# Cross-attention of a decoder block in turns of four heads: interleaved key and value chains, half-product queries, a ring of six PSUM banks

## The chip, the core and the metric

The kernel runs on one core of one Trainium2 chip. The metric is device time in microseconds (us) of one execution, the median of several runs. The engines, and how the profile names them: PE (TensorE, matmuls; PEld is its loading of weights), DVE (VectorE), ACT (ScalarE), POOL (GpSimd) and SP (SyncE, whose queue issues all the DMAs). Each engine takes its instructions in order and waits on semaphores for the others. PE writes its results into PSUM, which has 8 banks; the kernel gives a tile of PSUM one bank or more. Everything else lies in SBUF.

## The reference

The reference is one decoder block of three sublayers on `x` (8 batches, 224 rows, 512 columns), each followed by `x = layernorm(x + sublayer(x))`: a self-attention with normalised heads, a cross-attention over `ctx` (8 batches, 750 rows, 384 columns), and a gated feed-forward whose weights are rounded to -1, 0 and 1 times a scale. The change lies in the cross-attention:

```python
q = split_heads(x @ Wq)          # 16 heads of 64
k = split_heads(context @ Wk)
v = split_heads(context @ Wv)
sim = jnp.einsum('bhid,bhjd->bhij', q, k) * SCALE
attn = jax.nn.softmax(sim, axis=-1)
out = jnp.einsum('bhij,bhjd->bhid', attn, v)
return out.transpose(0, 2, 1, 3).reshape(b, sq, HEADS * DIM_HEAD) @ Wo + bo
```

All of it is in float32, but for the feed-forward's matmuls.

## The kernel before

The kernel has three stages: self-attention (to about 490 us), cross-attention (to about 1480 us) and feed-forward. In each stage the instructions of PE, DVE, ACT and POOL keep the order in which the source writes them (`manual_schedule`); the order of SP's queue is the framework's own, which also puts in all semaphore waits. A tile of a pool with one buffer may be written anew only when all its readers are done.

**Units.** The cross-attention runs over 64 units: 8 batches, and in each 8 pairs of heads (`units`, L1219). One pass of the loop at L1250 writes this order:

1. `scores` (L1060): for each of 6 chunks of 125 context rows and each of the two heads, one matmul of keys by queries. Two chunks of one head share a PSUM bank, so a unit takes 6 banks. ACT copies each bank to `cpT` (L1081), and from the second two chunks on DVE also reads the bank, for the running maximum (L1083). L1087 leaves the maximum per context row in `cmx`.
2. `across` (L1092): about a dozen small DVE instructions that take the maximum over the context rows, together with the sums of the unit before (`csm`), and leave the negated maxima and the inverse sums in `mx_n`. `negated_maxima` spreads the maxima over a PSUM bank.
3. one step of `weight_steps` (below).
4. `weighted` of the unit before (L1161): 12 matmuls of values by exponentials into one bank, `ov_c`.
5. the first part of a chain of products (`turn_products`): in odd passes the keys, in even ones the values, of four heads of one batch. A chain writes a 2 x 2 block matrix product as seven half-size products (`half_products`, L251) with a third inner block; it uses three PSUM banks, x, z and w, of which x is used four times over. ACT moves five of the results out, POOL adds two, DVE one (L301).
6. ACT's deferred half of the weight step (`acts`).
7. `queries` of the next unit (L1045): four matmuls of 224 columns, moved out by ACT with the scale.
8. `exponentials` (L1143): for each head DVE adds the negated maxima (L1147), ACT takes the exponential (L1155), POOL sums over the chunks (L1157 to L1159).
9. the rest of the chain, and then `normalise` of the unit before, which reads `ov_c` straight from PSUM (L1187).
10. loads of weight blocks for the next chains (`load_blocks`), context loads and sums a batch ahead, layernorm work, and the output projection of a finished tile of 128 rows (`cross_finish`, 16 matmul records of 512 columns).

**Banks.** The pool `c_mm` has 7 banks, handed out in order to score banks, spread maxima, queries, chain banks, transposes and projections; `ov_c` has the eighth.

**Weight steps.** The feed-forward's weights are brought in beside the cross-attention. In chunks of 2048 columns, two slots of `w_stage` in turn: first every chunk is loaded and its absolute values summed on ACT (L914); then every chunk is loaded again and in halves of 1024 columns scaled and rounded on ACT (L937), clipped on DVE (L940), converted on ACT (L947) and stored to DRAM (L948). One step goes with each unit, but for a few, until it is done.

**Weights.** All of `xattn_Wq` lies in SBUF. Blocks of key and value weights stream through `xw`, with sums of blocks that POOL formed during self-attention (`room_sums`, L138).

Of the kernel before, what the change touches and what calls it, by code (L numbers as in the profile page):

```python
# [38 lines left out]
HID = 2048  # L39
# [13 lines left out]
QH = 4  # L53
NCHUNK = 4
CHUNK = DIM * HID // P // NCHUNK
PIECE = 1024
# [9 lines left out]
def decoder_block(ctx: ExitStack, tc: tile.TileContext, a: dict, out: bass.AP):  # L66
# [95 lines left out]
    room_steps = room_sums(0), room_sums(1)  # L162
# [159 lines left out]
    with tc.tile_pool(name="a_sb", bufs=2) as sb, tc.tile_pool(  # L322
# [335 lines left out]
        ctx_even = xw = bo = None  # L658
# [3 lines left out]
        CTX = KC * SC + 4 * HALF  # L662
        contexts = {}

        def open_context(b, t):
            contexts[b] = (
                t[:, : KC * SC].rearrange("p (k r s) -> p k r s", k=KC, r=2),
                t[:, KC * SC :].rearrange("p (i s) -> p i s", i=4),
            )
# [7 lines left out]
        def sum_context(b, i):  # L677
# [4 lines left out]
                (s[:, 2], c[:, 0, 0], c[:, 0, 1], ALU.subtract),  # L682
                (s[:, 3], c[:, 1, 0], s[:, 1], ALU.subtract),
# [3 lines left out]
        def load_blocks(j, g):  # L687
# [8 lines left out]
            nc.sync.dma_start(out=xw[:, j, KC + 2 :], in_=sums_w[:, j, g])  # L696

# [28 lines left out]
        for m in range(NS):  # L726
# [25 lines left out]
            for _ in range({10: 1, 11: 1, 12: 1, 13: 2, 15: 1, 16: 1, 17: 1, 18: 2}.get(m, 0)):  # L752
                next(room_steps[m // 15])
            next(sums)
# [37 lines left out]
            if m == 13:  # L792
                room_load(1)
            if m == NS - 3:
# [4 lines left out]
                xwq = wpool.tile([P, KD, INNER], F32, tag="w", name="xattn_Wq")  # L799
# [4 lines left out]
                nc.sync.dma_start(  # L804
                    out=xwq, in_=a["xattn_Wq"].rearrange("(k p) n -> p k n", p=P)
                )
# [77 lines left out]
    with tc.tile_pool(name="c_sb", bufs=2, reuse_waits="tile") as sb, tc.tile_pool(  # L884
        name="c_mm", bufs=7, space=PSUM, reuse_waits="tile"
    ) as ps_mm, tc.tile_pool(
        name="c_ov", bufs=1, space=PSUM, reuse_waits="tile"
    ) as ps_ov, tc.manual_schedule(engines=ENGINES):
        ctx_odd = sb.tile([P, CTX], F32, name="ctx_odd", bufs=1)
# [5 lines left out]
        stage = sb.tile([P, 2, CHUNK], F32, name="w_stage", bufs=1)  # L895
        oT = sb.tile([P, NPAIR, RING], F32, name="coT", bufs=1)


        mx = sb.tile([P, 2, S], F32, name="cmx", bufs=1)
        nc.vector.memset(mx, -3.0e38)  # L900
        csm = sb.tile([P, 2, S], F32, name="csm", bufs=1)
        nc.vector.memset(csm, 0.0)
        xT = {}

        def stage_chunk(i, c, s):
            name = ("w_gateT", "w_upT", "w_downT")[i]
            kk = (HID // P if i == 2 else KD) // NCHUNK
            nc.sync.dma_start(
                out=stage[:, s, :].rearrange("p (k n) -> p k n", k=kk),
                in_=a[name].rearrange("(k p) n -> p k n", p=P)[:, c * kk : (c + 1) * kk, :],  # L910
            )
# [22 lines left out]
        def weight_round(i, c, s, h):  # L934

            piece = stage[:, s, h * PIECE : (h + 1) * PIECE]
# [3 lines left out]
            return lambda: nc.vector.tensor_scalar(  # L940
# [3 lines left out]
        def weight_store(i, c, s, h):  # L944
            piece = stage[:, s, h * PIECE : (h + 1) * PIECE]
            w = sb.tile([P, PIECE], BF16, name="w_t", bufs=1)
            nc.scalar.activation(w, piece, AF.Identity, bias=unrounder)  # L947
            nc.sync.dma_start(  # L948
                out=ternary[i][:, c, h * PIECE : (h + 1) * PIECE], in_=w
            )  # L950
# [9 lines left out]
        def weight_steps():  # L960
# [3 lines left out]
            for n, (i, c) in enumerate(chunks):  # L964
# [3 lines left out]
                acts.append(partial(weight_sum, i, c, n % 2))  # L968
# [3 lines left out]
            before = None  # L972
            for n, (i, c) in enumerate(chunks):
                for h in range(CHUNK // PIECE):
                    yield
                    if before:
                        weight_store(*before)
                    if h == 0 and n + 1 < len(chunks):
                        stage_chunk(*chunks[n + 1], (n + 1) % 2)
                    before = (i, c, n % 2, h)  # L980
                    acts.append(lambda at=before: late.append(weight_round(*at)))
            yield
            weight_store(*before)

        def transpose_x(b):

            for i in needs[b]:
# [5 lines left out]
                for pb, c, at, n in pieces(i):  # L993
                    if pb not in xT:
                        xT[pb] = sb.tile([P, KD, S], F32, name="xT")
                    nc.scalar.copy(xT[pb][:, :, c : c + n], tr[:, :, at : at + n])

        VN = QH * DH

        def products_kv(b, j, product, dest):

            c, sums = contexts[b]
            b11, b21, b31, b22, b32, t1, t2, t3, t4n, dif = (
                xw[:, j, i] for i in range(KC + 2 + NSUM)
            )
            like = lambda t: shaped(t, j)  # L1010
            part = lambda name: like(sb.tile([P, HALF + 9], F32, name=name, bufs=1))
            return half_products(
                product,
                [[c[:, k, r] for k in range(2)] for r in range(2)],
                ((b11, None), (b21, b22)),
                [sums[:, i] for i in range(4)],
# [233 lines left out]
        for n in range(-1, len(units)):  # L1250
# [12 lines left out]
            for f in acts:  # L1263
                f()
# [268 lines left out]
```

## Time and profile before

| quantity | value |
|---|---|
| median of 3 runs | 1639.58 us (1639.06 to 1640.03) |
| the profiled execution | 1638.94 us |
| its span, first to last instruction | 1637.2 us |
| granted TensorE clock, mean | 0.999 of full speed |
| busy PE, DVE, ACT, POOL | 1617.3, 1340.3, 984.7, 908.9 us |
| cross-attention, 495 to 1480 us: busy PE, DVE, ACT, POOL | 980.8, 813.7, 615.0, 571.6 us |
| PE start to start of a unit, value chain and key chain | 13.81 us (897.53 to 911.34), 13.53 us (911.34 to 924.87) |

The profile is a record of one execution. Busy time is the time in which an engine had an instruction under way; a matmul's end is modelled, so where matmuls follow each other the time from start to start is the better measure of one. A float32 matmul shows as two records. A line of a timeline gives the start, the duration, the engine, the source line, and what was written and read, and in brackets how long the engine had stood idle before and who ended that. Line numbers are those of the kernel before.

### The profile page before, as it was taken

What the parts mean: (1) busy time and instruction counts of PE and PEld (TensorE: products, weight loads), DVE (VectorE), ACT (ScalarE), POOL (GpSimd) and SP (SyncE); (2) the same over time, 40 slices, a digit from 0 to 9 for tenths busy, and PEclk for the clock granted to TensorE, in tenths of its full rate; (3) what the DMA queues carried; (4) which work ended last, traced back from release to release, by engine and by line L of the source; (5) the groups of instructions that cost most, each with busy time, mean ns of one, the idle gap of its engine ahead of it and who ended that gap; (6) DMA issues with size and microseconds to landing.
All of it is one profiled execution on the core that took longest, in us unless ns stands there. A gap on an engine that the chain in (4) does not pass through costs nothing.

```text
span 1637.2 us, 27209 instructions
## 1 busy us (share of the span) xinstructions
PE 1617.3 (99%) x9738; PEld 1145.1 (70%) x9738; DVE 1340.3 (82%) x2832; ACT 984.7 (60%) x1790; POOL 908.9 (56%) x805
## 2 busy tenths in 40 slices
PE   8999999999999999999999999999999999999998
PEld 5677666667747877876876876877776877864443
DVE  3999897879857887886886886998987887987877
ACT  5667455556416766764775775666655565655663
POOL 4886575545514555655665565565565565653244
PEclk9999999999999999999999999999999999999999
DMA  8115332313305333331332332232221131113343
GB/s 295 46 52 200 94 126 78 109 52 93 105 1 205 126 101 112 126 103 40 120 116 71 94 115 72 85 107 83 68 66 51 38 100 44 50 52 90 65 90 103
DMA packets 147462, 153.33 MB, mean 94 GB/s; under 512 B 41344, under 2 KB 113536, under 8 KB 144896
## 3 DMA queue, kind: packets, MB, share of 16 engines
q1 hardware_dynamic: 147328, 151.60, 29.7%
q8 instruction: 77, 1.26, 0.3%
q14 instruction: 57, 0.47, 0.1%
HBM read 126.14 MB, written 16.78 MB: 87 GB/s over the span
## 4 chain that ended last, share of the span: by engine, by line
PE 85%; DVE 9%; ACT 2%; issue 2%; DMA 0%; POOL 0%; SPq 0%; POOLq 0%; ACTq 0%; DVEq 0%
PE sc_c L1073 8%; PE ov_c L1167 8%; PE k_x L1034 6%; PE mm_o L646 6%; PE mm_co L239 6%; PE mm_f L1333 6%; PE v_x L1040 6%; PE mm_q L1049 5%; PE mm_v L521 5%; PE q_x L447 5%; PE k_w L1034 4%; PE v_w L1040 4%; PE ov_a L617 3%; PE sc_a L548 3%; PE q_w L447 2%
## 5 line engine op out<-in xcount | busy, mean ns | idle before, releaser
L1157 POOL TENSOR_TENSOR csh<-cpT 125x672 f32<-125x672 f32 x128 | 207.9, 1624 | 164.9 <-DVE cpT L1147 122.5
L1081 ACT COPY cpT<-sc_c 125x448 f32<-125x448 f32 x384 | 173.8, 562 | 76.2 <-PE sc_c L1073 74.8
L177 POOL TENSOR_TENSOR nm_i<-nm_q,mhalf 128x28 f32<-128x28 f32 x32 | 157.9, 4933 | 86.8 <-DVE nm_q L496 86.5
L1155 ACT ACTIVATE cpT<-cpT 125x1344 f32<-125x1344 f32 x128 | 169.1, 1323 | 51.7 <-DVE cpT L1147 44.6
L1147 DVE TENSOR_TENSOR cpT<-cpT,mx_b 125x1344 f32<-125x1344 f32 x128 | 193.2, 1551 | 2.2
L1073 PE MATMUL sc_c<-cqT,ckT 64*125 64x224 f32 x1536 | 173.8, 360 | 4.2 <-DVE cpT L1147 3.4
L1073 PEld LDWEIGHTS sc_c<-cqT,ckT 64*125 64x125 f32 x1536 | 143.6, 183 | 38.2 <-issue 22.4
L1167 PE MATMUL ov_c<-cpT,cv 125*64 125x224 f32 x1536 | 159.4, 357 | 0.0
L1167 PEld LDWEIGHTS ov_c<-cpT,cv 125*64 125x64 f32 x1536 | 104.8, 137 | 47.1 <-issue 10.3
L1083 DVE TENSOR_TENSOR cm<-sc_c,cpT 125x448 f32<-125x448 f32 x128 | 73.9, 619 | 73.7 <-ACT cpT L1081 73.7
L1049 PE MATMUL mm_q<-xT,xattn_Wq 128*128 128x224 f32 x512 | 107.3, 353 | 0.0
L1159 POOL TENSOR_TENSOR csm<-csm,csh 125x224 f32<-125x224 f32 x128 | 97.9, 765 | 10.0
L521 PE MATMUL mm_v<-wv,xnT 128*128 128x512 f32 x224 | 100.4, 592 | 0.0
L1049 PEld LDWEIGHTS mm_q<-xT,xattn_Wq 128*128 128x128 f32 x512 | 94.3, 190 | 8.1
L1158 POOL TENSOR_TENSOR csm<-csh 125x224 f32<-125x224 f32 x128 | 93.6, 731 | 10.0
L1333 PE MATMUL mm_f<-ternary,xqT 128*128 128x512 bf16 x448 | 98.5, 379 | 0.0
L239 PE MATMUL mm_co<-xattn_Wo,coT 128*128 128x512 f32 x224 | 98.5, 593 | 0.0
L259 ACT ACTIVATE pr<-sc_a 128x448 f32<-128x448 f32 x120 | 57.9, 535 | 64.4 <-PE sc_a L548 64.1
L572 DVE TRANSPOSE_TENSOR_REDUCE sm_q<-pr 128x28 f32<-128x896 f32 x64 | 70.6, 1103 | 19.7 <-ACT pr L259 19.3
L646 PE MATMUL mm_o<-attn_Wo,oT 128*128 128x512 f32 x192 | 84.3, 593 | 0.0
L1333 PEld LDWEIGHTS <-xqT 128*128 128x128 bf16 x448 | 43.8, 98 | 53.2 <-issue 0.6
L531 ACT ACTIVATE v<-mm_v,rms_rs 32x512 f32<-32x512 f32 (+2 forms) x80 | 54.4, 681 | 37.0 <-PE mm_v L521 36.3
(211 smaller groups left out, 3708.1 us busy)
## 6 DMA issues: line engine op xcount, KB each, us to landing
xw<-w_sums SPq DMA_DIRECT2D x64, 320.0 KB, 3.0
w_slot<-qk_sums SPq DMA_DIRECT2D x22, 512.0 KB, 3.6
w_stage<-w_gateT SPq DMA_DIRECT2D x8, 1024.0 KB, 5.2
w_stage<-w_upT SPq DMA_DIRECT2D x8, 1024.0 KB, 5.1
w_stage<-w_downT SPq DMA_DIRECT2D x8, 1024.0 KB, 5.5
xw<-xattn_Wk SPq DMA_DIRECT2D x32, 192.0 KB, 2.5
xw<-xattn_Wv SPq DMA_DIRECT2D x32, 192.0 KB, 2.5
tern<-w_t SPq DMA_DIRECT2D x24, 256.0 KB, 2.0
```

The costliest lines, as they stand in the source:

```text
L239: nc.tensor.matmul(mm, lhsT=oT[:, k, c : c + P], rhs=w[:, k, :], start=(k == 0), stop=(k == NPAIR - 1),)
L521: nc.tensor.matmul(mm, lhsT=xnT[:, k, at : at + P], rhs=wv[:, k, c * 512 : (c + 1) * 512], start=(k == 0), stop=(k == KD - 1),)
L646: nc.tensor.matmul(mm, lhsT=joint[g][:, hp, :] if at < 0 else o[:, at : at + P], rhs=wo[:, hp, :], start=(hp == 0), stop=(hp == NPAIR - 1),)
L1034: nc.tensor.matmul(mm, lhsT=w, rhs=c, start=start, stop=True, skip_group_check=True)
L1049: nc.tensor.matmul(mm, lhsT=xwq[:, k, hp * P : (hp + 1) * P], rhs=xT[:, k, :], start=(k == 0), stop=(k == KD - 1),)
L1073: nc.tensor.matmul(sc[j][:, i, :], lhsT=kT[h0 : h0 + DH, ct * CT : (ct + 1) * CT], rhs=qT[h0 : h0 + DH, :], start=True, stop=True,)
L1081: nc.scalar.copy(pT[:, j, 2 * c2 : 2 * c2 + 2, :], sc[j])
L1147: nc.vector.tensor_tensor(pT[:, j], pT[:, j], nm[:CT, j] .rearrange("p (o q) -> p o q", o=1) .to_broadcast([CT, NCT, S]), ALU.add,)
L1155: nc.scalar.activation(pT[:, j], pT[:, j], AF.Exp)
L1157: nc.gpsimd.tensor_tensor(half, pT[:, j, 0:3], pT[:, j, 3:6], ALU.add)
L1167: nc.tensor.matmul(ov[h0 : h0 + DH, :], lhsT=v[:, ct, hq * DH : (hq + 1) * DH], rhs=pT[:, j, ct, :], start=(ct == 0), stop=(ct == NCT - 1),)
L1333: nc.tensor.matmul(mm, lhsT=xqTs[i][:, k, :], rhs=w[:, k, cols], start=(k == 0), stop=(k == KD - 1),)
```

## The change

The 64 units become 32 turns, each of four heads of one batch; a turn takes the even or odd batch of a pair, and the pair's two batches take the same four heads one after the other, so blocks of weights serve two turns.

- **Order of a turn.** `weighted` of the turn before comes first, then `scores` of both pairs of heads, `across` for all four heads at once, and the maxima subtracted for the first pair. Then a key chain (of the next turn) and a value chain (of this turn) are dealt out step by step, one and the other (`half_steps`, a generator with a yield after each product). The first pair's exponentials stand behind the fifth step of each, the second pair's maxima behind the seventh key step, its exponentials behind the last product, and then `normalise`.
- **Weighted values** of two pairs of heads go into the two halves of one bank, each copied to SBUF by ACT (`ov_s`); `normalise` reads that copy.
- **Queries** are computed in every second turn for two turns, as seven half-size products over the pair of batches, at the end of the turn. Their weight blocks and sums of blocks stream in (`load_queries`); POOL forms the sums during self-attention (`room_query_sums`, passes 20 to 23), and sums of `xT` in this stage (`sum_x`). The scale moves to the copy of the transposes, which are made for two batches at once (four tiles; two tiles are made twice).
- **Banks.** `c_mm` has 6, the spread maxima get one of their own, `ov_c` has the eighth.
- **Weight steps** work on chunks of 1024 columns (`NCHUNK` 8), one step at the end of every turn and one at the start of the next, each with its ACT work in place.
- **Smaller.** Most pools have one buffer; contexts are loaded at the end of the turns that free their buffer; the sums of a context take three blocks, one replacing context rows; the last four tiles' layernorm work, not the last three's, lies in the feed-forward stage.

```diff
-QH = 4
-NCHUNK = 4
+NCHUNK = 8
...
+    def room_query_sums():
+
+        blk = room.rearrange("p (h k g c n) -> p h c k g n", h=2, k=2, c=2, n=P)
+        b = lambda h, c: blk[:, h, c]
+        for n, y, p, q in (
+            (0, b(0, 0), b(0, 1), b(0, 0)),
+            (2, b(0, 1), b(1, 1), b(0, 1)),
+            (1, b(1, 1), b(1, 1), b(0, 0)),
+            (3, b(1, 0), b(1, 0), b(1, 1)),
+        ):
+            for k in range(2):
+                nc.gpsimd.tensor_tensor(y[:, k], p[:, k], q[:, k], ALU.subtract)
+                nc.sync.dma_start(out=sums_xq[:, :, n, k], in_=y[:, k])
+            yield
...
-        name="c_mm", bufs=7, space=PSUM, reuse_waits="tile"
+        name="c_mm", bufs=6, space=PSUM, reuse_waits="tile"
     ) as ps_mm, tc.tile_pool(
+        name="c_nm", bufs=1, space=PSUM, reuse_waits="tile"
...
+            for n, at in enumerate(chunks):
+                yield
+                if n:
+                    weight_store(*chunks[n - 1], (n - 1) % 2)
+                if n + 1 < len(chunks):
+                    stage_chunk(*chunks[n + 1], (n + 1) % 2)
+                weight_round(*at, n % 2)
...
+        def half_steps(product, a, b, sums_a, sums_b, dest, part, acc, third=None):
...
+            m1, x_ = part("m1"), acc("x")
+            product(x_, a11, b11, True)
+            nc.scalar.copy(m1, x_)
+            yield
+            z_ = acc("z")
+            product(z_, a12, b21, True)
+            if third:
+                product(z_, a13, b31, False)
+            nc.scalar.copy(c11, z_)
+            nc.gpsimd.tensor_tensor(c11, c11, m1, ALU.add)
+            yield
+            u2 = part("u2")
+            product(x_, s2, t2, False)
+            nc.scalar.copy(u2, x_)
+            yield
...
+        def weighted(t, pTs):
+
+            v = vs.pop(t)
+            ov = ps_ov.tile([P, 2, S], F32, name="ov_c")
+            out = sb.tile([P, 2, S], F32, name="ov_s")
+            for w in range(2):
+                for ct in range(NCT):
+                    for j in range(2):
+                        h0, hq = j * DH, 2 * w + j
+                        nc.tensor.matmul(
+                            ov[h0 : h0 + DH, w, :],
...
+                nc.scalar.copy(out[:, w], ov[:, w])
+            return out
...
+        for t in range(-1, TURNS):
+            next(steps, None)
+            if t >= 1:
+                ov = weighted(t - 1, prior)
+            if t >= 0:
+                pTs = scores(t)
+                res = across(t == 0, False)
+                less_maxima(0, pTs[0], res)
+            ks = kv_steps(t + 1, 0) if t + 1 < TURNS else iter(())
+            vals = kv_steps(t, 1) if t >= 0 else iter(())
+            for _ in range(5):
+                next(ks, None)
+                next(vals, None)
+            if t >= 0:
+                exponentials(0, pTs[0])
+            next(ks, None)
+            next(vals, None)
+            next(ks, None)
+            if t >= 0:
+                less_maxima(1, pTs[1], res)
+            next(ks, None)
+            next(vals, None)
+            next(vals, None)
+            if t >= 0:
+                exponentials(1, pTs[1])
+            if t >= 1:
+                normalise(t - 1, ov, res)
+            prior = pTs
+
+            p, g, u = place(t + 1)
+            if t % 2 and t + 1 < TURNS:
+                for _ in query_steps(t + 1):
+                    pass
+                if t + 3 < TURNS:
+                    load_queries(place(t + 3)[1])
+            if t >= 0 and t % (2 * QG) == 2 * QG - 2 and t + 2 < TURNS:
+                transpose_x(t // (2 * QG) + 1)
+            for i in done.get(t, ()):
+                cross_finish(i)
+            for f in jobs.get(t, ()):
                 f()
...
+            next(steps, None)
+
+            if t % 2 == 0 and t + 2 < TURNS:
+                load_blocks(0, place(t + 2)[1])
+            if t % 2 and 0 < t and t + 1 < TURNS:
+                load_blocks(1, place(t + 1)[1])
```

## The prediction

> **What bounds the kernel now.** I read the page first, then busy time by stage, then the cross-attention stage engine by engine over two units, then the DMA issues.
>
> ```profile
> PE 1617.3 (99%) x9738; PEld 1145.1 (70%) x9738; DVE 1340.3 (82%) x2832; ACT 984.7 (60%) x1790; POOL 908.9 (56%) x805
> ...
> PE 85%; DVE 9%; ACT 2%; issue 2%; DMA 0%; POOL 0%; SPq 0%; POOLq 0%; ACTq 0%; DVEq 0%
> ```
> ```profile
> 495.00:1480.00 985.00, 980.76 (x6656) 751.76 (x6655) 813.67 (x1679) 615.02 (x1052) 571.63 (x559) 1.00 0.28 89
> ```
> The windows' columns are the stretch, its length, busy time of PE, PEld, DVE, ACT, POOL, then clock, DMA share and GB/s. TensorE is the bound: in the stage that changes, it is idle 4.2 of 985 us. So removed matmuls count in full, and so does every wait put in front of a matmul.
>
> ```profile
> 897.53 2.54 PE L1073 MATMUL sc_c<-cqT,ckT 64*125 64x224 f32 x24
> 900.00 2.49 PE L1167 MATMUL ov_c<-cpT,cv 125*64 125x224 f32 x24
> 902.42 0.92 PE L1040 MATMUL v_x<-xw,ctx_odd 128*125 128x128 f32 x6
> ...
> 907.11 1.68 PE L1049 MATMUL mm_q<-xT,xattn_Wq 128*128 128x224 f32 x8
> 908.62 1.47 PE L1040 MATMUL v_w<-xw,ctx_odd 128*125 128x128 f32 x12
> 911.34 2.54 PE L1073 MATMUL sc_c<-cqT,ckT 64*125 64x224 f32 x24
> ```
> These rows give start, duration, engine, line, operation. Start to start: scores 2.47, weighted values 2.42, queries 1.51, a value chain 7.41 (the same list gives 7.13 for a key chain). Weighted values are issued behind the next unit's scores, so the exponentials have those 2.5 us more to finish:
>
> ```profile
> 909.12 2.68 ACT L1155 ACTIVATE cpT<-cpT 125x1344 f32<-125x1344 f32 x2
> 911.71 0.46 ACT L305 COPY cv<-v_x 125x384 f32<-125x384 f32 x1
> 912.45 2.71 ACT L1081 COPY cpT<-sc_c 125x448 f32<-125x448 f32 x6 [0.28 <-PE sc_c L1073]
> 913.88 1.16 DVE L1083 TENSOR_TENSOR cm<-sc_c,cpT 125x448 f32<-125x448 f32 x2 [1.13 <-ACT cpT L1081]
> 915.00 1.20 ACT L947 ACTIVATE w_t<-w_stage,unrounder 128x1024 bf16<-128x1024 f32 x1
> 916.64 0.38 SPq L908 DMA_DIRECT2D w_stage<-w_upT  x1
> ```
> Exponentials end at 911.8, wanted at 913.80: 2 us spare. A weight load is issued only after the store that empties its slot (ended 916.2).
>
> **The change, part by part.** A turn is two units' work.
>
> *Gain.* Per two turns queries fall from 16 to 14 matmuls of 1.51/4 = 0.378 us: 16 x 2 x 0.378 = 12.1 us. Transposed tiles rise from 14 to 16 (0.52 each): +1.0. In the self-attention stage POOL gets 8 subtractions of 512 columns (nearest row L1198, 1.26): 10 us, hidden, as POOL is busy 285 of 495 us there; that is the price if it isn't. Block loads halve (192 to about 96 issues), query loads add 48; the DMA share is 0.28, so none. The unwaited turn on PE: 4.84 weighted + 4.94 scores + 14.54 chains = 24.3; an odd turn has 14 x 0.378 = 5.3 of queries more.
>
> *Ring of six.* Scores take 12 banks in a row; VectorE frees one in 0.58 us (1.16 for two) where PE fills one in 0.41 (2.47 for six). PE meets a full ring twice in the second pair, about 0.3 each: 0.6 a turn, none to 1.2.
>
> *ACT's tail.* Let E be the end of the turn's last value product. The second pair's exponentials are now queued on ACT behind that product's eviction: 0.46 + 2.68, so ACT is free at E+3.1. VectorE, from the start of scores: first maximum 2.54, maxima 2 x 2.88, across 3.7 + 1.0 (reductions of 896 columns at 1.10 against 0.65 and 0.60), three steps 3.63 + 0.54 + 3.63: 20.8, where E is 5.5 + 14.5 = 20.0. So DVE is not later than ACT; value c21 follows at E+1.3 and normalise (1.95) at E+3.3, which frees ov_s.
>
> *Weighted values now lead the turn, evicted by ACT in halves.* PE does the first pair E to E+2.7 (held 0.25 by c21). Both halves lie in one bank. The row at 913.88 shows what that means: DVE could read sc_c and the first copy was long done, but it started exactly when ACT's third copy, of the same bank, ended (912.45 + 2 x 0.43 + 0.56). So I take it that the second pair's matmuls wait for the first half's copy (0.35, as L1057).
> Even turn: copy 3.3, second pair 3.75 to 6.2, against 4.84: 1.35, with the ring 1.95.
> Odd turn: the third query product reuses the bank that m1's copy empties, and that copy stands behind the exponentials: it starts at 3.5, not 1.5, and five products of 0.757 end at 7.3 instead of 5.3; first pair, copy and second pair reach 12.65 against 10.14: 2.5, with the ring 3.1. Behind the second pair PE holds the next turn's scores and chains, and behind the late copy ACT holds twelve score copies, so nothing makes the time up.
>
> *POOL and SP.* POOL's partial sums take 3.45 a head (L1157 to L1159) from the first exponential on and end 30.3 after the scores began; the next turn's across wants them at 33 or later: hidden, by 3. Context loads move to the end of the turns that free their buffer, every eighth and the one behind: 5.9 to land, then 4 x 0.9 on POOL behind its partial sums, at E+14, wanted by the third key product at about E+16: hidden, or some 4 us at each of 3 pair changes if POOL is late.
>
> *Weight steps.* One stands at each turn's end and one at the next turn's start, so on ACT two run back to back, ahead of the first half's copy.
> Sums (turns 0 to 11): 2 x 1.15 (half of L914's 1.91, plus 0.19). Even: ACT 5.4, second pair 5.8 to 8.25: 3.4 + 0.6 = 4.0. Odd: 2.7 + 0.6 = 3.3. If the load waits on SP behind query blocks that free only with the last query product (no row shows it), it is 4 more in each uncovered odd turn (0.8 to issue, 3.6 and more to land, less the cover); I take none, since SP's queue in the trace is not in source order (L696 goes before L693).
> Rounds (turns 12 to 23): store 1.20 at the turn's end, then its slot's load is issued 0.45 later and takes 3.6:
>
> ```profile
> w_slot<-qk_sums SPq DMA_DIRECT2D x22, 512.0 KB, 3.6
> ...
> tern<-w_t SPq DMA_DIRECT2D x24, 256.0 KB, 2.0
> ```
> then the next round (1.24), then the copy. Even: 3.1 + 1.2 + 4.05 + 1.24 + 0.35 = 9.95; second pair 10.0 to 12.45: 7.6 + 0.6 = 8.2. Odd, from ACT free at 7.7: to 17.0 against 10.14: 6.9 + 0.6 = 7.5. In the kernel before, one step per unit sits between key or value evictions, with a unit (13.7) for its load.
>
> *Cover.* Output projections (6.87 a tile) fall at the end of turns 7, 8, 15, 16, 23, 24, 31; there only ring, copy and, if odd, query wait remain: about 14 in all.
> Sum: sums 5 x 4.0 + 5 x 3.3 = 36; rounds 5 x 8.2 + 4 x 7.5 = 71; no step 3 x 1.95 + 3 x 3.1 = 15; covered 14: 136 us.
>
> *Clock.*
> ```profile
> 1623.65 7.07 PE L1421 MATMUL dn<-ternary,hqT 128*128 128x512 bf16 x32
> ...
> 1632.00:1634.00 2.00, 0.00 (x0) 0.00 (x0) 1.49 (x5) 0.00 (x0) 0.78 (x1) 1.00 0.02 7
> 1634.00:1638.00 4.00, 0.00 (x0) 0.00 (x0) 0.09 (x1) 0.00 (x0) 0.00 (x0) 0.51 0.33 128
> ```
> PE ends at 1630.7 and the clock is half from about 1634. The nine uncovered round turns hold PE for 7.3 or 4.85 us, so the second pair may run at half clock: 0 to 2.4 us each; the middle, 11 us.
> The Trainium skill (TensorE: Matmul & The Clock Gate, "What's actually happening") has half rate after an idle window of about 3.4 us, as the row, and full rate only after as much busy time: an estimate from its figures is 1.7 a turn, 15 us for my 11.
>
> Against the profiled execution's 1638.9 (span 1637.2 + 1.7): 1638.9 - 12.1 + 1.0 + 136 + 11 = 1775. The runs' median is 0.6 above that execution: 1775.
>
> **The rule that speaks against the change.** Without the wait on the shared bank, the second pair waits only for its exponentials (E+3.15), and ACT's lateness reaches PE six score banks later: sums 1.3 even and 2.6 odd, rounds 4.4 and 4.2, no step as sums, covered 9.5: 20 + 39 + 12 + 9.5, with the gain 1708.
> The Trainium skill (PSUM — Partial Sum Buffer, "Terms") says that two engines on one bank and quadrant at once are an error, reads against reads included. By it the copy has to be waited for, 1775; by a tracker that sees only halves, 1708.
>
> **Rivals.**
> *Halves are told apart*: 1708. For: PE reads ckT's first half while ACT writes its second (L305 at 925.42 beside scores from 924.87), so SBUF halves are told apart. Against: the row at 913.88.
> *The short tail*: no bank wait, weight loads in time, ACT free 1 us earlier. Left are the ring and 1.0 of query wait: 13 even turns x 0.6, 12 odd x 1.6, covered 8, in all 35 on 1628: 1663. For: the row's rounds and stores are hidden now. Against: the load can't be issued before the store that empties its slot.
> *Faster*: PE never waits. 1638.9 - 12.1 + 1.0 = 1628. Place: the start of weighted values. It decides if the added wait is below 11/32 = 0.35 us a turn, which needs the exponentials to end before E+2.4. For: 99% PE now with the same work per engine. Against: their 2.68 us come after E.
> *Longer*: loads queue on SP (+16) and the clock costs 2.4 each (+11): 1802.
>
> **How the numbers follow.** Likeliest (with Longer) 0.62, halves 0.20, short tail 0.12, faster 0.05, the rest between. The range runs from under the halves' case to above Longer: 1685 to 1815, leaving short tail and faster out; the likeliest alone, 1735 to 1815. A measurement tells 0.2% (3 us): faster 0.05, within 0.01, slower 0.94.
>
> **What would show it.** PE idle ahead of the second pair's weighted values, ended by ACT's copy of ov_c: about 1 us in turns without a step, 7 in even round turns; idle before the third query product, 2 us; ACT idle before the round, ended by the w_stage DMA; the stage's PE busy time down by 11 us and its length up by over 100. PE at 99% with none of these, or waits only at scores, would prove me wrong.

## The result, and the profile after

The changed kernel takes 1800.41 us (median of four executions, 1797.21 to 1802.68); the kernel before, on the same chip, 1639.32 us. The ratio is 1.098, with a 95% interval of 1.0961 to 1.0999. The prediction was 1775 us, in a range of 1685 to 1815.

The page of the changed kernel, the lines that answer to those shown of before:

```profile
span 1797.8 us, 26691 instructions
PE 1653.3 (92%) x9668; PEld 1152.6 (64%) x9682; DVE 1297.4 (72%) x2388; ACT 1024.5 (57%) x1906; POOL 944.4 (53%) x861
...
PEclk9999999999999999999999899988999999999999
...
PE 75%; DVE 9%; ACT 8%; issue 4%; DMA 2%; POOL 1%; SPq 0%; POOLq 0%; ACTq 0%; DVEq 0%
...
L1307 PE MATMUL ov_c<-cpT,cv 125*64 125x224 f32 x1536 | 185.2, 395 | 95.3 <-ACT ov_s L1314 90.7
```

Of the kernel before, the clock row and the same group:

```profile
PEclk9999999999999999999999999999999999999999
...
L1167 PE MATMUL ov_c<-cpT,cv 125*64 125x224 f32 x1536 | 159.4, 357 | 0.0
```

TensorE's share of the span fell from 99% to 92%, and ScalarE's part of the chain that ended last rose from 2% to 8%. The last line of each view is the group of the weighted values: 95.3 us of idle time now stand ahead of them, 90.7 of which end with ScalarE's copy of the first half; before there was none. Their mean is 395 ns a record instead of 357, and TensorE's clock row shows 8s in the middle, where before it had nines only. Stage by stage (the columns are stretch, length, busy time of PE, PEld, DVE, ACT, POOL, then clock):

```profile
495.00:1640.00 1145.00, 1017.65 (x6597) 758.28 (x6596) 767.01 (x1242) 654.73 (x1168) 597.64 (x608) 0.96 0.23 72
```

The cross-attention stage was 985 us long with 981 us of work on TensorE; it is now 1145 us long, with 1018 us recorded as busy, at a mean clock of 0.96. What TensorE waited for (total us, times, longest), in the whole execution:

```profile
PE ov_c L1307 <- ACT ov_s L1314: 90.7, 32, 8.8
PE mq_x L1077 <- ACT xwq L1095: 25.8, 15, 1.7
...
PE mm_co L262 <- DVE coT L1332: 5.0, 1, 5.0
PE ov_c L1307 <- DVE cv L1123: 4.6, 9, 0.5
```

In the kernel before, the longest of them in this stage were seven waits ahead of scores:

```profile
PE sc_c L1073 <- DVE cpT L1147: 3.4, 7, 1.3
```

Once in every turn, 32 times, the second pair of weighted values waits for ScalarE; in 15 turns the third query product does. Turn 18, an even turn with a rounding step, shows how. These are TensorE, ScalarE and SyncE from the end of the turn's last value product, 1160.77:

```profile
1160.77 1.36 PE L1307 MATMUL ov_c<-cpT,cv 125*64 125x224 f32 x12
1162.63 1.36 PE L1307 MATMUL ov_c<-cpT,cv 125*64 125x224 f32 x12 [0.50 <-DVE cv L1123]
1171.04 4.10 PE L1307 MATMUL ov_c<-cpT,cv 125*64 125x224 f32 x24 [7.05 <-ACT ov_s L1314]
1175.07 5.83 PE L1202 MATMUL sc_c<-cq,ckT 64*125 64x224 f32 x48
```
```profile
1161.26 2.54 ACT L1291 ACTIVATE cpT<-cpT 125x1344 f32<-125x1344 f32 x2
1163.70 1.13 ACT L992 ACTIVATE w_t<-w_stage,unrounder 128x1024 bf16<-128x1024 f32 x1
1164.74 1.23 ACT L983 ACTIVATE w_stage<-w_stage,rounder,wscale 128x1024 f32<-128x1024 f32 x1
1167.38 1.15 ACT L992 ACTIVATE w_t<-w_stage,unrounder 128x1024 bf16<-128x1024 f32 x1 [1.42 <-DMA tern<-w_t]
1169.52 1.24 ACT L983 ACTIVATE w_stage<-w_stage,rounder,wscale 128x1024 f32<-128x1024 f32 x1 [0.99 <-DMA w_stage<-w_upT]
1170.66 0.32 ACT L1314 COPY ov_s<-ov_c 128x224 f32<-128x224 f32 x1
```
```profile
1165.28 0.38 SPq L957 DMA_DIRECT2D w_stage<-w_upT  x1
```

The first pair is done at about 1164. Its copy, L1314, has ahead of it on ScalarE the second pair's exponentials, a store and a round, and then a second store and a second round, each of which first waits for a DMA. So it starts at 1170.66, and TensorE's second pair at 1171.04. That pair then takes 4.10 us instead of 2.49, and the scores behind it 5.76 us from start to start (1175.07 to 1180.83) instead of the 4.94 of two units before.

### The profile page after: what moved, and what is told of

It is laid out like the page before. It is cut to its first block, busy times and chain, and to the rows that moved or that the text cites. A ratio compares the mean times of both kernels' runs of the same rounds, so it can differ in the third digit from the quotient of the medians.

```text
span 1797.8 us, 26691 instructions
## 1 busy us (share of the span) xinstructions
PE 1653.3 (92%) x9668; PEld 1152.6 (64%) x9682; DVE 1297.4 (72%) x2388; ACT 1024.5 (57%) x1906; POOL 944.4 (53%) x861
## 4 chain that ended last, share of the span: by engine, by line
PE 75%; DVE 9%; ACT 8%; issue 4%; DMA 2%; POOL 1%; SPq 0%; POOLq 0%; ACTq 0%; DVEq 0%
PE sc_c L1202 9%; PE ov_c L1307 7%; PE mm_co L262 5%; PE mm_f L1472 5%; PE k_x L1064 5%; PE v_x L1070 5%; PE mm_v L544 5%; PE q_x L470 5%; PE mm_o L669 5%; PE v_w L1070 4%; PE k_w L1064 4%; ACT cpT L1291 3%; PE ov_a L640 2%; PE sc_a L571 2%; PE mq_x L1077 2%
## 5 line engine op out<-in xcount | busy, mean ns | idle before, releaser
L1307 PE MATMUL ov_c<-cpT,cv 125*64 125x224 f32 x1536 | 185.2, 395 | 95.3 <-ACT ov_s L1314 90.7
L1102 POOL TENSOR_TENSOR ckT<-ckT,xwq 128x375 f32<-128x375 f32 x32 | 31.3, 978 | 355.8 <-ACT ckT L1101 355.8
L1307 PEld LDWEIGHTS ov_c<-cpT,cv 125*64 125x64 f32 x1536 | 115.3, 152 | 160.2 <-ACT ov_s L1314 103.6
L1279 DVE TENSOR_TENSOR cpT<-cpT,mx_b 125x1344 f32<-125x1344 f32 x128 | 193.2, 1551 | 2.2
L1202 PE MATMUL sc_c<-cq,ckT 64*125 64x224 f32 x1536 | 190.2, 370 | 0.6 <-ACT cpT L1210 0.5
L1202 PEld LDWEIGHTS sc_c<-cq,ckT 64*125 64x125 f32 x1536 | 153.1, 187 | 39.2 <-DVE cm L1212 24.7
L1314 ACT COPY ov_s<-ov_c 128x224 f32<-128x224 f32 x64 | 21.7, 340 | 159.0 <-PE ov_c L1307 156.7
L1295 POOL TENSOR_TENSOR csm<-csh 125x224 f32<-125x224 f32 x128 | 85.9, 671 | 10.0
L1296 POOL TENSOR_TENSOR csm<-csm,csh 125x224 f32<-125x224 f32 x128 | 84.4, 659 | 10.0
L1117 POOL TENSOR_TENSOR ckT<-ckT,cku 128x375 f32<-128x375 f32 x32 | 31.4, 983 | 109.1 <-ACT cku L1116 109.1
L262 PEld LDWEIGHTS mm_co<-xattn_Wo,coT 128*128 128x128 f32 x224 | 42.8, 193 | 56.4 <-issue 50.6
```

Of the source, the lines that this page charges most:

```text
L262: nc.tensor.matmul(mm, lhsT=oT[:, k, c : c + P], rhs=w[:, k, :], start=(k == 0), stop=(k == NPAIR - 1),)
L1202: nc.tensor.matmul(sc[j][:, i, :], lhsT=kT[h0 : h0 + DH, w, ct * CT : (ct + 1) * CT], rhs=q[h0 : h0 + DH, t % 2, w], start=True, stop=True,)
L1279: nc.vector.tensor_tensor(pT[:, j], pT[:, j], nm[:CT, j] .rearrange("p (o q) -> p o q", o=1) .to_broadcast([CT, NCT, S]), ALU.add,)
L1307: nc.tensor.matmul(ov[h0 : h0 + DH, w, :], lhsT=v[:, ct, hq * DH : (hq + 1) * DH], rhs=pTs[w][:, j, ct, :], start=(ct == 0), stop=(ct == N ...
```

## The experiments

All of them are the changed kernel with an edit. Ratios are to the kernel before, with 95% intervals.

**One copy behind both pairs.**

```diff
-                nc.scalar.copy(out[:, w], ov[:, w])
-            return out
+            nc.scalar.copy(out, ov)
+            return out
```

> The changed kernel with one copy of both halves of ov_c behind all 24 matmuls, in place of one copy per half. Theory (the second pair's matmuls wait for the copy of the first half, because both lie in one bank): the waits of PE ended by the copy to ov_s (90.7 us in the changed kernel's trace) go. The second pair then waits only for its exponentials: turns without a weight step lose 1.5 (even) and 0.5 us (odd), turns of sums 3 and 0.5, turns of rounds 5.5 and 4, because ACT's late work then holds the scores' banks instead: about 1800 - 75 = 1725, between 1700 and 1745, with the idle time of PE now ahead of scores and ended by ACT. Rival (PE is held by ACT as such, through banks or exponentials, and would be at the next place too): 1785 or more.

Measured: 1722.08 us, ratio 1.0503 (1.0482 to 1.0524). TensorE's longest waits:

```profile
PE mq_x L1077 <- ACT xwq L1095: 29.1, 15, 5.0
PE sc_c L1202 <- ACT cpT L1210: 23.9, 10, 4.6
```

With no copy between the pairs, the wait at the second pair is gone; what is left of ScalarE's lateness reaches TensorE only behind the six banks of scores, and but for one wait of 0.5 us in the first turn only in turns with rounding steps (nine waits). The copy in the middle, with what stands ahead of it, cost 78 of the 161 us.

**Two banks for the two halves.**

```diff
-            nm = ps_nm.tile([P, 2, S], F32, name="mx_b")
+            nm = sb.tile([P, 2, S], F32, name="mx_b", tag="rc")
...
-            ov = ps_ov.tile([P, 2, S], F32, name="ov_c")
+            ov = [ps_ov.tile([P, S], F32, name=f"ov_c{w}") for w in range(2)]
...
-                nc.scalar.copy(out[:, w], ov[:, w])
+                nc.scalar.copy(out[:, w], ov[w])
```

> Edit: the changed kernel with the two halves of the weighted values in two banks, each half still copied by ScalarE as soon as its 24 matmuls are done; the bank for the second half comes from the spread maxima, which VectorE now writes to SBUF instead of PSUM. It asks whether the 90.7 us ahead of the second pair are due to the shared bank or to ScalarE's two copies as such. My theory, the shared bank: the wait before the second pair goes, ScalarE's lateness reaches TensorE only at the scores, and the time is near that of the run with one copy behind both pairs (1722 us): 1710 to 1750, the upper part for VectorE's additions, which now read both operands from SBUF beside GpSimd. The rival, that the order on ScalarE alone holds the second pair: 1785 us or more.

Measured: 1824.22 us, ratio 1.1122 (1.1104 to 1.1141). The mechanism came out as expected and the time did not; it lies where the rival had put it. No wait of the weighted values for ScalarE's copy is left, though the copy is where it was in ScalarE's order: the shared bank made that wait. But the price of the bank was larger than what it bought:

```profile
PE mq_x L1075 <- ACT xwq L1093: 62.8, 15, 7.3
PE ov_c L1305 <- DVE cv L1121: 31.2, 13, 3.0
PE sc_c L1200 <- ACT cpT L1208: 22.7, 11, 5.0
PE mm_co L262 <- DVE coT L1330: 10.7, 4, 6.6
```

VectorE's addition of the spread maxima is the first group here, and the second is the same one in the changed kernel (busy us, mean ns):

```profile
L1277 DVE TENSOR_TENSOR cpT<-cpT,mx_b 125x1344 f32<-125x1344 f32 x128 | 269.8, 2147 | 2.2
```
```profile
L1279 DVE TENSOR_TENSOR cpT<-cpT,mx_b 125x1344 f32<-125x1344 f32 x128 | 193.2, 1551 | 2.2
```

With both operands in SBUF an addition takes 2147 ns on average, with one in PSUM 1551 (the last section shows that this goes with GpSimd's work beside it). Four of them a turn make VectorE 2.4 us later, and the exponentials behind it too. The waits fit that: the one for m1's copy is 3.95 us in most odd turns instead of 1.72, the one for c21 3.0 us in most even turns instead of 0.5, and together they grow by 64 us. The four lines above come to 127 us, those of the changed kernel to 126, so the waits only moved; and TensorE's clock was granted at 0.965 on average, against 0.976.

**The two weight steps moved into the turn.** One stands behind the first pair's maxima, one behind the first pair's exponentials, so that they are no longer back to back ahead of the copy. `clips()` issues a step's part on VectorE, which is held back until then; the second one's stands behind `normalise`.

```diff
-            next(steps, None)
             if t >= 1:
                 ov = weighted(t - 1, prior)
...
                 less_maxima(0, pTs[0], res)
+            next(steps, None)
+            clips()
...
                 exponentials(0, pTs[0])
+            next(steps, None)
...
-            next(steps, None)
             if t % 2 == 0 and t + 2 < TURNS:
```

> The changed kernel with its two weight steps of a turn moved off the turn's ends: one behind the copies of the scores, one behind the first pair's exponentials; the second one's clip on VectorE stands behind normalise. Theory (two steps back to back ahead of the copy, the second waiting for a load that is issued behind the first's store): even turns of rounds fall from about 36 to 28 us, odd ones from 40 to 33.5, even turns of sums from 29.3 to 27.2: 1800 - 78 = 1722, between 1705 and 1740. All turns then look like those without a step, with waits of 1.4 to 0.4 us for the copy. Rival (ACT has no room in the middle of a turn, and holds the chains' banks there instead): 1765 or more, with PE idle ahead of the third and later products of the chains.

Measured: 1749.12 us, ratio 1.0668 (1.0647 to 1.0689): above the range and below the rival's 1765.

```profile
PE mq_x L1081 <- ACT xwq L1099: 47.5, 16, 5.5
PE ov_c L1311 <- ACT ov_s L1318: 25.4, 32, 1.7
```

The wait at the second pair did fall from 90.7 to 25.4, and the uncovered even turns with rounding are 27.5 to 28.7 us long from scores to scores, about as I had expected; but the query wait grew from 25.8 to 47.5. In turns 13, 17, 19 and 21 it grew by 1.1 us each, where the step behind the first exponentials pushes the second ones back; in turns 7, 11, 15 and 23 by 2.0 to 3.4 (in turn 7 ScalarE had already waited 3.76 us for VectorE ahead of the first exponentials); and a new wait of 5.5 us stands ahead of the first scores.

**Dummy work in the wait.** Five fp32 products of 512 columns with nothing to wait for, between the pairs of nine turns; they add to the work and take a bank of the ring each time; all else stays as it is.

```diff
+                if w == 1 and t in (12, 13, 14, 17, 18, 19, 20, 21, 22):
+                    idle = ps_mm.tile([P, DIM], F32, tag="mm", name="idle")
+                    for _ in range(5):
+                        nc.tensor.matmul(idle, lhsT=ident, rhs=xwo[:, 0, :], start=True, stop=True)
```

> The changed kernel with five float32 matmuls of 512 columns (0.43 us a record, 4.3 us in all), whose result nobody reads, between the two pairs of weighted values in nine turns of rounds (those of 12, 13, 14 and 17 to 22). Nothing else changes. Theory (part of the loss is TensorE's clock, which falls to half in the waits of 5 to 9 us, so that the second pair takes 3.7 to 4.7 us and not 2.4): PE is then idle under 3.3 us at a time in these turns, the pair takes 2.4 again, and the added work makes the kernel faster by 9 x 1.8 = 16 us: 1784, between 1778 and 1792. Rival (the pair is slow after a wait for another reason, such as weights that have to be loaded anew): 1800 or more.

Measured: 1790.45 us (1788.43 to 1792.77), ratio 1.0925 (1.0907 to 1.0943). The kernel with more work is 10 us faster than the one without. The same turn as above:

```profile
1159.23 4.56 PE L1307 MATMUL idle<-xattn_Wo,ident 128*128 128x512 f32 x10
1166.48 2.49 PE L1313 MATMUL ov_c<-cpT,cv 125*64 125x224 f32 x24 [2.69 <-ACT ov_s L1320]
```

The pause is 2.69 us instead of 7.05, and the second pair takes 2.49 us instead of 4.10. So part of the loss is not the wait but the clock behind it. In three of the nine turns (12, 20 and 22) pauses of 2.69, 4.31 and 2.80 us were left, and the pair still took 4.17 to 4.75 us.

**Weighted values and scores dealt out by pairs.** First pair of weighted values, first pair of scores, then the second ones: the copy has 2.5 us of scores beside it, and VectorE empties six banks before the next six are wanted.

```diff
-                ov = weighted(t - 1, prior)
...
-                pTs = scores(t)
+            wt = weighted(t - 1, prior) if t >= 1 else iter(())
+            sc = scores(t) if t >= 0 else iter(())
+            next(wt, None)
+            next(sc, None)
+            for _ in range(2):
+                ov = next(wt, None)
+                pTs = next(sc, None)
```

> The changed kernel with weighted values and scores dealt out by pairs of heads: first pair weighted, first pair's scores, second pair weighted, second pair's scores. Work and all else are the same. Theory: 2.5 us of scores cover the copy and the tail of the second pair's exponentials, and VectorE catches up between the two pairs' scores, so the 0.8 us a turn that PE loses at a full ring of banks goes as well. Turns without a step fall from 27.2 to 25 and from 32.8 to 31.4 us, turns of sums from 29.3 to 25.6 and 32.8 to 31.4, turns of rounds by about 3: 1800 - 73 = 1727, between 1705 and 1745. Rival (VectorE's chain is the limit, which starts 2.5 us later for the second pair): its end moves the exponentials back by as much, and it stays above 1780.

Measured: 1723.43 us, ratio 1.0511 (1.049 to 1.0532).

```profile
PE ov_c L1309 <- ACT ov_s L1316: 34.2, 14, 6.3
PE mq_x L1077 <- ACT xwq L1095: 29.1, 15, 5.0
PE sc_c L1203 <- POOL cq L1102: 14.4, 12, 1.6
```

Eighteen of the 32 second-pair waits are gone, and the ring's with them: 24 score records take 2.47 us from start to start, 4.94 a turn instead of 5.77. A new wait appeared: the first scores now follow the queries more closely than GpSimd's last addition into them.

**Queries ahead of the second exponentials.** In turns with query products, `exponentials(1, ...)` is issued behind them.

```diff
-            if t >= 0:
+            if t >= 0 and not (t % 2 and t + 1 < TURNS):
                 exponentials(1, pTs[1])
...
                 for _ in query_steps(t + 1):
                     pass
+                if t >= 0:
+                    exponentials(1, pTs[1])
```

> Edit: in the 15 turns with query products, the second pair's two exponentials are issued behind the query products instead of ahead of them; nothing else. It asks whether ScalarE's order alone makes the query wait (25.8 us, 15 waits of 1.72 us in the changed kernel) and whether that wait is worth its 26 us. My theory: the wait of m1's copy goes to under 5 us in sum, but the second exponentials then begin 1.5 to 2.5 us later against the end of the turn, and ScalarE's copy of the next turn's first weighted values with them, so the wait ahead of the second pair grows by about as much in these turns: 1800 us give or take 12 (1788 to 1812). The rival, the prediction's own sum, in which the query wait stands as a term that falls away by itself: 1770 to 1780 us.

Measured: 1804.0 us, ratio 1.1007 (1.0988 to 1.1025).

```profile
PE ov_c L1307 <- ACT ov_s L1314: 114.1, 32, 8.8
...
PE mq_x L1077 <- ACT cku L1106: 0.7, 1, 0.7
```

The query wait was due to ScalarE's order, and removing it alone is worth nothing: 25.8 us leave one line and 23.4 come back in the other, since the copy of the first half now stands behind exponentials that begin later.

**The four orders together.** Pairs, steps in the middle, queries first, as above, and the last value half product's addition (c21) ahead of the second maxima on VectorE:

```diff
             next(ks, None)
+            next(vals, None)
             if t >= 0:
                 less_maxima(1, pTs[1], res)
             next(ks, None)
             next(vals, None)
-            next(vals, None)
```

> Edit: four orders changed together, no arithmetic: weighted values and scores dealt by pairs (as in the run with pairs, 1723 us), the two weight steps of a turn put behind the first pair's maxima and behind the first pair's exponentials (as in the run with the steps in the middle, 1749 us), the second pair's exponentials behind the query products, and the last value half product's addition ahead of the second pair's maxima on VectorE. My theory, that the loss is made of waits on ScalarE's order and not of the work itself: 1800 less 91 for the second pair, 25 for the ring, 26 for queries and some 15 of the clock gives 1643, with residues 1630 to 1660 us. The rival, that the changed arrangement has a floor of its own (VectorE at 72% and ScalarE's chain of two pairs of exponentials per turn) and waits only move: 1690 us or more.

Measured: 1658.04 us, ratio 1.0113 (1.0098 to 1.0128). The first three alone moved the time by -77, -51 and +4 us, which adds to 124; together, with the addition, it is 142. The addition alone was not run, so how much of the other 18 us is its own stays open. The longest waits left in the cross-attention stage:

```profile
PE mq_x L1081 <- ACT xwq L1099: 20.5, 7, 5.4
...
PE mm_co L262 <- DVE coT L1338: 5.4, 1, 5.4
...
PE sc_c L1207 <- DVE cm L1217: 2.7, 1, 2.7
PE ov_c L1313 <- ACT ov_s L1320: 1.8, 3, 0.7
```

**Projections in front of the queries.** To that kernel, three more moves; their core:

```diff
+                if t in done:
+                    exponentials(1, pTs[1])
+                    for i in done.pop(t):
+                        cross_finish(i)
+                    for _ in query_steps(t + 1):
+                        pass
...
+            if t == TURNS - 1:
+                for i in done[t]:
+                    cross_project(i, 0, NPAIR - 2)
+                for i in done.pop(t):
+                    cross_project(i, NPAIR - 2, NPAIR)
+                    cross_add(i)
...
-                n += (i - i0) % 2
+                n += 1 if i0 == 0 else (i - i0) % 2
```

> Edit: the four orders together (the run at 1658 us) and three more moves: in turns 7, 15 and 23 the finished tiles' output projections stand ahead of the query products instead of behind them (there the query products waited 3.0, 4.6 and 4.65 us); in the last turn the projections of the four tiles run their first six head pairs for all tiles before the last two (there a wait of 5.4 us on the normalised values); and the normalisation of finished tiles goes one tile per turn instead of two on VectorE (there a wait of 2.7 us ahead of the scores of turn 21). My theory, that TensorE's work in the changed arrangement is short enough and only waits stand above it: 1658 less 12.3, 5.4, 2.7 and about 5 of the clock behind these waits gives 1633, range 1628 to 1642, so it would be level with the kernel before or up to 0.7% faster. The rival, that such waits come back elsewhere as the second weight step's did: 1650 us or more.

Measured: 1645.19 us, ratio 1.0039 (1.0025 to 1.0052): above the range, though below the rival's 1650.

```profile
PE mm_co L262 <- DVE coT L1338: 9.7, 4, 3.4
PE mq_x L1081 <- ACT xwq L1099: 9.0, 5, 5.5
```

The query waits of turns 7, 15 and 23 went, and 2.7, 3.3 and 3.4 us of waiting for normalised values, which stand behind the second maxima on VectorE, took their place. The longest one left, 5.5 us, lies ahead of the first scores; it was there in the run before, and I had overlooked it.

**The last two moves.** The split of the projections for turns 7, 15 and 23 as well, and one weight step instead of two ahead of the first scores.

```diff
             if t >= 0:
                 exponentials(0, pTs[0])
-            next(steps, None)
+                next(steps, None)
...
-                    for i in done.pop(t):
-                        cross_finish(i)
+                    for i in done[t]:
+                        cross_project(i, 0, NPAIR - 2)
+                    for i in done.pop(t):
+                        cross_project(i, NPAIR - 2, NPAIR)
+                        cross_add(i)
```

> Edit: as the run at 1645 us, and two more moves: the projections in turns 7, 15 and 23 too run their first six head pairs for all their tiles before the last two (there waits of 2.7, 3.3 and 3.4 us on the normalised values of the turn before), and the turn ahead of the first scores takes one weight step instead of two (there the query products waited 5.5 us for ScalarE, whose queue stood behind the sum of a chunk still on its way). My theory, that no floor but these waits is left above TensorE's own work: 1645 less 9.4 and 5.5 and 2 to 3 of the clock gives 1628, range 1624 to 1634, so faster than the kernel before by 0.3 to 0.9%. The rival, that the changed arrangement can only be made level: 1639 us or more.

Measured: 1637.22 us against 1639.32 (11 and 15 executions), ratio 0.9979 (0.997 to 0.9988): faster than the kernel before by 0.2%, but 3 us above my range.

```profile
PE mm_co L262 <- DVE coT L1338: 6.4, 3, 3.5
...
PE ov_c L1313 <- ACT ov_s L1320: 4.1, 5, 2.0
PE mq_x L1081 <- ACT xwq L1099: 3.6, 4, 0.9
```

The wait ahead of the first scores is gone and so is the one in turn 15, where four tiles give 24 matmuls to run first. Turns 7 and 23 have two tiles; their twelve matmuls only fill the time up to the same wait (2.72 and 3.45 us). Four of the executions took 1633.5 to 1634.0 us (granted clock 0.998), seven 1636.7 to 1638.0 (0.995 or 0.996). The profiled one is of the seven, and has this in turn 12, where the weight means are worked out:

```profile
882.55 4.17 PE L1313 MATMUL ov_c<-cpT,cv 125*64 125x224 f32 x24 [1.97 <-ACT ov_s L1320]
```

The wait and the slow pair are 1.97 + 1.68 = 3.65 us, which is about the distance of the two groups. But a stretch of 3.41 us at half clock, as behind this wait, lowers the mean of an execution by 0.001, and the groups differ by 0.002 or 0.003, so this turn is not shown to be the difference; there is no trace of the first group.

## Why the prediction was right, and where it was not

The direction, the mechanism and the range held; the time was 25 us too low. The sum from the trace, as a difference of spans (160.6): waits of the weighted values 90.7 + 4.6, query wait 25.8, ring 26.6, the wait on coT 5.0, clock 23.8, gain -17; together 159.5. Against the prediction's terms the clock is 13 us larger, the waits of the weighted values 8 (its terms for them come to about 87), the ring 7 and the end of the stage 5; the gain is 6 us larger too and the query wait 4 smaller, so part of the errors cancelled, and the total is closer by that luck. What it put at nothing for GpSimd and for the loads of weight blocks and contexts held: TensorE's list shows no wait for either in this stage.

- **Weighted values lead the turn, evicted in halves in one bank.** Right. In turn 18 the copy ends at E + 10.21 (predicted 9.95), and the second pair starts at E + 10.27 (predicted 10.0). The wait is 95.3 us in all, with 4.6 for c21. By kind: even turns with rounding waited 7.05 to 8.77, odd ones 5.1 to 6.2, even ones with sums mostly 2.16, odd ones 0.44. The rival *halves are told apart* (1708) fell: TensorE waited for the copy in all 32 turns, and with two banks that wait was gone. The Trainium skill (PSUM — Partial Sum Buffer, "Terms") has two engines on one bank and quadrant at once as an error; the kernel's waits go by that rule, here at a price of 78 us against one copy.
- **Query wait.** Predicted 2.0 in each odd turn; measured 1.72, 25.8 in all. The run with queries first shows its cause, ScalarE's order.
- **Ring of six.** Predicted 0.6 a turn; scores took 5.77 us instead of 4.94, so 0.83, or 26.6 instead of 19.
- **Clock.** The step that failed most in size: 11 us, the middle of 0 to 22. In thirteen turns the second pair took 3.83 to 4.75 us instead of 2.49, 23.8 us in all, just above my upper bound. The nine uncovered turns with rounding lost 2.0 each instead of my 1.2; the other four (turns 2, 6, 10 and 23) followed waits of only 2.16 to 2.88 us, and I had left them out of this term. The dummy products took back 10 us. (My estimate from the Trainium skill, TensorE: Matmul & The Clock Gate, "What's actually happening", was 15.)
- **Cover.** I let only ring, copy and query wait remain in the turns with projections, 14 us. In turns 15, 16 and 23 the second pair waited 2.71, 2.71 and 2.46 us. I had not followed VectorE: the weight step's clip (L986) stands there behind the addition of the projected tile, which waits for TensorE, and the next store on ScalarE waits for the clip. These waits of ScalarE lie beside TensorE's projections for the most part, and what is left of them reaches the copy:

```profile
ACT w_t L992 <- DVE w_stage L986: 41.3, 6, 13.7
```

- **The end.** I had nothing for the last turn. Its projections waited 5.0 us for normalised values behind the second maxima; the kernel before, where another tile's projections stand in that place, has no such wait.
- **Gain.** Predicted 12.1 less 1.0. Where nothing waits (the four orders together), an even turn takes 24.13 us and an odd one 29.43, on average 26.78; two units before took 27.34. Over 32 turns that is 17.9, less 1.0. The alternated chains take 14.35 us (24.13 less 4.94 of scores and 4.84 of weighted values) instead of 14.54, which I had carried over unchanged. My sign for it, busy time of the stage down by 11 us, was a bad one: matmuls at a lower clock are longer, and it rose from 981 to 1018.
- **Short tail** (1663), **faster** (1628) and **longer** (1802): the time lies at *longer*, but by half of its mechanism: the clock did cost 24 us, while the loads were not late in odd turns with sums, whose second pairs waited 0.44 us; that the ring, the covered turns and the end make up the rest is chance. *Short tail* fell with the wait on the bank, and its loads were not in time: in turn 18 the second round waited 0.99 us for one. *Faster* was no error of the arithmetic: with the order of the issues mended, the same work runs in 1637.

## What to carry to other kernels

When a rearrangement lets one engine's operations follow each other more closely, walk the queue of every engine that has to answer in between, in program order, and write down what stands ahead of the one instruction that TensorE waits for. A short copy between two halves of one bank inherits everything that is queued in front of it, here up to 8.8 us for 0.34 us of work. Mend all the orders before judging the arrangement: one at a time, three of them were worth 77, 51 and -4 us, and together with a fourth 142.

## What the runs showed of the hardware

A pause of two microseconds can cost TensorE its clock. Over eight traces (the changed kernel and all runs but those with one copy and with two banks), these are the second pairs of weighted values by the pause ahead of them; a pair is 24 records and takes 2.49 us at full clock (the other 103 pairs had no pause and were not slower):

| pause, us | pairs | at 2.49 us | slower (3.57 to 4.75) |
|---|---|---|---|
| under 1.0 | 68 | 68 | 0 |
| 1.0 to 1.9 | 27 | 26 | 1 |
| 1.9 to 3.0 | 33 | 15 | 18 |
| 4.3 to 8.8 | 25 | 0 | 25 |

Between 1.9 and 3.0 us it goes either way, for the same pause in the same place: a wait of 2.16 us was followed by 3.89 us in turn 2 of the changed kernel and by 2.49 in turn 4. The clock's records show what goes with it. In the changed kernel the stretches at a clock of 0.5 last 3.41, 6.83 or 10.24 us (but for the last, which the end of the record cuts off), and all fifteen begin on one grid of 3.41 us; in every other trace with more than one they lie on such a grid too. Turn 2's pause falls for the most part into one stretch of the grid, turn 4's is divided between two (columns as above):

```profile
590.66:594.07 3.41, 1.36 (x12) 0.77 (x12) 2.64 (x4) 3.41 (x5) 3.17 (x4) 1.00 0.00 0
594.07:597.48 3.41, 2.88 (x16) 1.93 (x18) 0.00 (x0) 0.48 (x3) 3.17 (x4) 0.50 0.71 228
652.10:655.51 3.41, 1.92 (x18) 0.92 (x14) 3.27 (x5) 3.41 (x5) 3.17 (x4) 1.00 0.00 0
655.51:658.92 3.41, 2.23 (x24) 1.63 (x24) 0.00 (x0) 1.12 (x3) 3.17 (x4) 1.00 0.60 183
```

In turn 2 TensorE is idle for 2.05 us of the first stretch (1.63 of the pause, the rest of the short wait inside the first pair), and the next one runs at half clock; in turn 4 for 1.49 and 1.18 us, and the clock stays. Of the 153 pauses in the table, 43 of the 44 with a slower pair behind them had at least 1.97 us of idle time within one stretch (the other 1.89), and the 109 others at most 1.98. So it is the idle time within a stretch that tells, and in these traces a pause of 2 to 3 us left the clock at full speed only where the grid divided it. This is read off the traces; no run was made to shift a pause on the grid. The Trainium skill (TensorE: Matmul & The Clock Gate, "What's actually happening") speaks of an idle window of about 3.4 us; the stretches agree with that length, but a pause of 1.9 to 3.0 us was enough in 18 of 33 cases, so here the measurement decides.

An addition on VectorE of 125 x 1344 fp32 took 1551 ns on average with its second operand in PSUM and 2147 ns with it in SBUF. The operand's place does not do that alone. With it in SBUF, 34 of the 128 additions took 1551 to 1560 ns; the other 94 took 1791 to 2968 ns, and GpSimd was at work for 73% of their time or more. With it in PSUM, in the changed kernel, none took more than 1556 ns, though GpSimd was at work for at least half the time of 125 of them.
